# Averages over the channels from two float32r halves, and the next block's v product placed later: a retention and FFN layer on one Trainium2 core

## The chip, the cores and the metric

The kernel runs on one core of one Trainium2 chip (trn2). The metric is the device time of one execution in microseconds (us): the median of several runs, and beside it one execution taken with the hardware profiler. The engines are called as in the profile: PE is the matrix engine, PEld its weight load, DVE the vector engine, ACT the scalar engine, POOL GpSimd, and SP the engine whose queue issues nearly all DMAs.

## The reference, cut to what matters

The input has 4 sequences of 1024 tokens with 512 channels. All is float32; the FFN weights are first rounded to float8_e4m3fn.

```python
x = L0_attn_x
x = x + _layernorm(_L0_attn_ref(_layernorm(x), Wq, Wv, Wo, Wg, gamma, beta_ln, beta))
x = x + _layernorm(_L0_ffn_ref(_layernorm(x), gate_w, up_w, down_w, scales...))

# _L0_attn_ref(x)
q = (x @ Wq.T).reshape(Bsz, Ls, NHEAD, HEAD_DIM)
v = (x @ Wv.T).reshape(Bsz, Ls, NHEAD, HEAD_DIM)
ret = _retention_scan(v, lam)              # state = lam * state + v_t along the tokens
out = (q * ret).reshape(Bsz, Ls, D)
out = _layernorm(out, ln_gamma, ln_beta)   # mean and variance over the 512 channels
out = out * jax.nn.silu(x @ Wg.T)
return out @ Wo.T

# _L0_ffn_ref(x)
fuse = silu((x @ q8(gate_w)) * gate_scale) * ((x @ q8(up_w)) * up_scale)
return (fuse @ q8(down_w)) * down_scale
```

The change touches the mean and the variance of the inner `_layernorm(out, ...)`, and the order in which one v product is issued.

## The kernel before, in words

**Tiles.** The 4096 tokens are cut into 8 blocks of 512. For the attention half of a block (`class Retention`, line 316 and on) activations lie with channels on the 128 partitions: 512 channels are 4 chunks (`c`), and a tile of one chunk is 128x512. Each of q, v and g (`gate` of `Retention`, line 451) takes for each chunk four f32 products of 128x512 that add up in one PSUM tile (`project`, line 281). In the profile one f32 product is two rows. The scan along the tokens is one DVE instruction for each chunk (`scan`, line 393). `y_of` (line 412) multiplies q by the scanned v, and POOL adds the four chunks into `self.sum` (`ysum` in the profile).

**Mean and variance over the channels.** Channels lie on partitions and over four chunks. After POOL has summed the chunks, one f32 product with a 128x128 matrix of 1/512 (`mean_w`) sums over the partitions and gives each partition the mean (`mean`, line 425, PSUM tile `mu`). `center_y` (line 429) subtracts it from the four chunks on DVE, squares them on ACT, and POOL adds up the squares (`sqsum`). `var` (line 442) does the same product on these, and ACT takes the root; `rstd_y` (line 448) inverts it on DVE. `z` (line 465) then scales a chunk, shifts it and multiplies it by silu(g); `o` (line 477) is the output product.

**The FFN half** (`class Ffn`, line 533 and on) goes through 12 steps `i` of 128 inner channels. `gate` and `up` do eight float32r products each: the input was split into two float32r halves, an upper one made by an ACT cast and the rest by a DVE subtraction (`upper_of`, `rest_of`, lines 525 and 528), and each is multiplied by the rounded weights. `fuse` (line 557) multiplies gate and up on DVE and casts the upper half on ACT, `rest` subtracts the other half on DVE, and `down` does eight products two steps later.

**The order.** Every operation goes through `InOrder` (line 66), which keeps the program order on each engine; so every row of the profile names line 74, and rows are told apart by their tiles. The order is written out by hand in the loop of line 784: loop `t` runs the FFN of block t (`f`), and weaves into its 12 steps the rest of the FFN of block t−1 (`l`), the attention of block t+1 (`b`, there in loops 0 to 6) and the loading, normalizing and first products of block t+2 (`n`, there in loops 0 to 5). In steps 3 to 6 PE does `f.gate(i)`, then a group of g for `b`, then `f.up(i)`, then `f.down(i-2)`. In step 3 the mean of `b` stands ahead of that group, in step 4 the variance. In step 11 the first v chunk of `n` follows `f.gate(11)`.

```python
            if n and i == 11:
                n.v(0)
                n.scan(0)
            if n and i == 11:
                b.turn_x1n(3)
                b.upper_of(3)
            units()
            f.up(i)
            f.fuse(i)
```

The normalized input of `n` reaches this product through memory: DVE transposes 32x32 blocks (`send_x`, line 366), a DMA writes them (`mx`), and `fetch_x` (line 380, issued at the end of step 9, or 7 in loop 0) reads them back into `xnT`. The transposed FFN input of `b` goes a like way for three of four token groups (`move_x1n`); the fourth is turned on PE (`turn_x1n(3)`, tile `pt`). Loop 0 also rounds the FFN weights to float8 on DVE and ACT (`rounds`, line 221, and `units`, line 214; tiles `scr`). Loop 1 looks for weights out of range on ACT (`next(search)`; tile `seen`).

**Buffers.** PSUM: tag `pa` has two buffers, which v, q, g, mu, var, o and the transposes take in turn; `pf` has two for gate and up; `pd0` to `pd3` have one each for down. In SBUF, tag `ret` has two buffers (scanned v, squares, blocks to be transposed, search), tag `rstd` one (`ysum`, then `sqsum`, then the root), tag `sg` three (gates).

Of the kernel before, what the change touches and what calls it, by code (L numbers as in the profile page):

```python
# [10 lines left out]
F32 = mybir.dt.float32  # L11
I32 = mybir.dt.int32
F32R = mybir.dt.float32r
F8 = mybir.dt.float8e4
AF = mybir.ActivationFunctionType
ALU = mybir.AluOpType

P = 128
# [5 lines left out]
def retention_ffn_sandwich(  # L24
# [24 lines left out]
    TB = 512  # L49
# [5 lines left out]
    const = ctx.enter_context(tc.tile_pool(name="const", bufs=1))  # L55
# [3 lines left out]
    work = ctx.enter_context(tc.tile_pool(name="work", bufs=2))  # L59
# [6 lines left out]
    class InOrder:  # L66
# [9 lines left out]
    pe, dve, act, pool, sp = (  # L76
        InOrder(e) for e in (nc.tensor, nc.vector, nc.scalar, nc.gpsimd, nc.sync)
    )
# [49 lines left out]

    ident = const.tile([P, P], F32, tag="ident", name="ident")
    make_identity(nc, ident)  # L130
    mean_w = const.tile([P, P], F32, tag="mean_w", name="mean_w")
    dve.memset(mean_w, 1.0 / D)
    eps_sb = const.tile([P, 1], F32, tag="eps_sb", name="eps_sb")
    dve.memset(eps_sb, EPS)
# [79 lines left out]
    def units():  # L214

        while open_units:
            _, c = open_units.pop(0)
            act.activation(c, c, AF.Relu, bias=neg_low)
            act.activation(c, c, AF.Identity, scale=1.5 * 2.0**20, bias=low_unit)
# [41 lines left out]
    def rstd_in_place(var, n):  # L261
        pool.tensor_scalar(var, var, EPS, 1.0, ALU.add, ALU.mult)
        pool.tensor_tensor(var, var, nhalf[:, :n], ALU.pow)
# [30 lines left out]
    def ps_tile(name, home="pa"):  # L294
        return homes[home].tile([P, TB], F32, tag=home, name=name)
# [20 lines left out]
    class Retention:  # L316
# [24 lines left out]
        def shift(self):  # L341

            mean, rstd = self.mv[:, :, 0], self.mv[:, :, 1]
            pool.tensor_scalar(mean, mean, -1.0, 1.0, ALU.mult, ALU.mult)
            pool.tensor_tensor(mean, mean, rstd, ALU.mult)
# [76 lines left out]
                pool.tensor_tensor(self.sum, self.sum, y[:, c, :], ALU.add)  # L422


        def mean(self):
            self.mu = ps_tile(f"mu_{self.t}")
            pe.matmul(self.mu, mean_w, self.sum, start=True, stop=True)

        def center_y(self):

# [10 lines left out]

        def var(self):
            var = ps_tile(f"var_{self.t}")
            pe.matmul(var, mean_w, self.sum, start=True, stop=True)
            self.sum = work.tile([P, TB], F32, tag="rstd", name=f"rstd_{self.t}", bufs=1)
            act.activation(self.sum, var, AF.Sqrt, bias=eps_sb)

# [226 lines left out]
    b = Retention(1)  # L674
# [109 lines left out]
    for t in range(NB):  # L784
        f, n = Ffn(a), None
        for i in range(NI):
            if t > 0 and (t > 1 or i):
                (f if i else l).rest((i - 1) % NI)
            if t == 0 and i == 0:
                n = Retention(2)  # L790
# [44 lines left out]
            if l and b and i == 2:  # L835
                l.stats(0)
                l.stats(1)
            if b and i == 3:
                b.mean()
                b.center_y()  # L840
                if t == 0:
                    n.stats(3)
                    n.rstd()
                    n.shift()
                b.g_of(0)
            if b and i == 4:
                b.var()
                b.g_of(1)
                b.rstd_y()
            if b and i == 5:  # L850
                b.g_of(2)
                b.z(1)
# [14 lines left out]
                b.upper_of(i - 9)  # L867
            if b and 7 <= i <= 10:
                b.o_moments(i - 7)
            if n and i == 11:  # L870
                n.v(0)
                n.scan(0)
            if n and i == 11:
                b.turn_x1n(3)
                b.upper_of(3)
            units()
            f.up(i)
            f.fuse(i)
            if t == 0:
                if i < 8:  # L880
                    rounds(3, now=i == 3)
# [57 lines left out]
            if b and i == 4 and 0 < t < NB - 2:  # L939
                n = Retention(t + 2)  # L940
# [6 lines left out]
        l, a, b = f, b, n  # L947
# [70 lines left out]
```

## Time and profile before

| what | value |
|---|---|
| median of 3 runs | 1018.72 us (1018.16 to 1019.34) |
| the profiled execution, its own time | 1018.71 us |
| its span (first to last instruction) | 1016.9 us |
| TensorE clock granted, mean | 0.997 of full speed |
| DVE busy | 605.7 us in 931 instructions |
| ACT busy | 321.4 us in 475 instructions |
| POOL busy | 242.7 us in 290 instructions |
| g products (pg<-xnT,wg_sb), rows, busy | 256, 114.9 us |
| mu and var products, rows | 16 and 16 |

A row of the timeline has the start (from the span's start), the duration, the engine, the line, the operation with output and inputs, the shape and a count; the bracket at its end is idle time of the engine just before and what ended it. Rows of PE overlap, since products are pipelined: the cost of a group in a full stream is the distance from the end before to its own end. A row of waits gives the total, the number and the longest. The profiled execution is within the spread of the runs, and 1.8 us longer than its span.

### The profile page before, as it was taken

The page shows a single profiled execution, that of the slowest core. Times are in us where ns is not written, and L with a number is a line of the kernel's source. Part 1 is how long each engine was busy: PE and PEld are TensorE (multiplying, and loading weights), DVE is VectorE, ACT ScalarE, POOL GpSimd, SP SyncE. Part 2 cuts the span into 40 slices and gives each one's busy share as a digit, 9 for nine tenths or more (in the row PEclk, how much of TensorE's full clock was granted, in tenths as well). Part 3 has the DMA queues.
Part 4 walks back from the last instruction along what each step waited for, and adds up shares of the span by engine and source line. Part 5 has one row for each costly group of instructions (what it writes and reads, how often), then busy time and mean ns, then how long its engine had stood idle before and what let it go on. Part 6 is the DMA issues. An engine that isn't in the chain of part 4 may idle for free.

```text
span 1016.9 us, 9749 instructions
## 1 busy us (share of the span) xinstructions
PE 995.9 (98%) x3502; PEld 651.0 (64%) x3502; DVE 605.7 (60%) x931; ACT 321.4 (32%) x475; POOL 242.7 (24%) x290
## 2 busy tenths in 40 slices
PE   9999999999999999999999999999999999999997
PEld 6454766666665666666666566665666666666885
DVE  5996896435665465753657446573556735547444
ACT  3646574334754132111321113211141111412222
POOL 1405222214031140311413114130132302213021
PEclk9999999999999999999999999999999999999998
DMA  9212224301125022340204402052020510103021
GB/s 302 103 61 103 84 83 104 103 1 51 43 83 135 0 86 91 103 114 1 83 11 121 96 1 83 18 135 76 0 83 32 134 63 1 42 21 124 1 83 41
DMA packets 62608, 73.79 MB, mean 73 GB/s; under 512 B 5856, under 2 KB 36320, under 8 KB 62560
## 3 DMA queue, kind: packets, MB, share of 16 engines
q1 hardware_dynamic: 60976, 72.24, 23.2%
q10 hardware_dynamic: 1584, 0.94, 0.4%
q8 instruction: 27, 0.44, 0.2%
q14 instruction: 21, 0.17, 0.1%
HBM read 43.53 MB, written 29.62 MB: 72 GB/s over the span
## 4 chain that ended last, share of the span: by engine, by line
PE 87%; DMA 5%; DVE 4%; POOL 2%; ACT 1%; issue 1%; SPq 1%; POOLq 0%; DVEq 0%; ACTq 0%
PE pfu L74 16%; PE pfg L74 15%; PE pd L74 15%; PE pv L74 11%; PE pg L74 10%; PE pq L74 10%; PE po L74 8%; DMA xnT<-mx 3%; DVE xn L74 1%; DMA mx<-xn 1%; PE var L74 1%; PE mu L74 1%; SPq L74 1%; POOL x L74 1%; POOL sqsum L74 1%
## 5 line engine op out<-in xcount | busy, mean ns | idle before, releaser
L74 PE MATMUL pfu<-x1nT,up_sb 128*128 128x512 f32 x768 | 222.0, 431 | 0.0
L74 PE MATMUL pfg<-x1nT,gate_sb 128*128 128x512 f32 x768 | 190.4, 390 | 1.2 <-ACT x1nT L74 0.7
L74 PE MATMUL pd<-down_sb,fuse 128*128 128x512 f32 x720 | 188.3, 403 | 0.0
L74 PEld LDWEIGHTS pfu<-x1nT,up_sb 128*128 128x128 f32 x768 | 144.1, 188 | 61.1 <-issue 35.2
L74 PEld LDWEIGHTS pfg<-x1nT,gate_sb 128*128 128x128 f32 x768 | 143.9, 188 | 31.7 <-DVE x1nT L74 1.0
L74 PEld LDWEIGHTS pd<-down_sb,fuse 128*128 128x128 f32 x720 | 135.2, 188 | 38.0 <-issue 10.8
L74 ACT CAST fuse<-gate 128x512 fp32r<-128x512 f32 x90 | 55.9, 621 | 306.9 <-DVE gate L74 306.9
L74 DVE SCALAR_TENSOR_TENSOR gate<-pfu,us_sb,gate 128x512 f32<-128x512 f32 x96 | 71.7, 747 | 122.4 <-PE pfu L74 118.3
L74 ACT ACTIVATE gate<-pfg,gs_sb 128x512 f32<-128x512 f32 x96 | 65.9, 686 | 246.6 <-PE pfg L74 243.5
L74 PE MATMUL pv<-xnT,wv_sb 128*128 128x512 f32 (+1 forms) x280 | 115.2, 557 | 8.6 <-DMA xnT<-mx 7.0
L74 PE MATMUL pg<-xnT,wg_sb 128*128 128x512 f32 x256 | 114.9, 592 | 0.0
L74 PE MATMUL pq<-xnT,wq_sb 128*128 128x512 f32 x256 | 114.9, 592 | 0.0
L74 PE MATMUL po<-wo_sb,y 128*128 128x512 f32 x256 | 114.5, 592 | 0.0
L74 POOL TENSOR_SCALAR mv<-mv 128x1 f32<-128x1 f32 (+1 forms) x77 | 19.8, 257 | 331.2 <-DVE mv L74 330.5
L74 PEld LDWEIGHTS pv<-xnT,wv_sb 128*128 128x128 f32 x280 | 52.4, 189 | 57.2 <-issue 43.3
L74 PEld LDWEIGHTS pg<-xnT,wg_sb 128*128 128x128 f32 x256 | 48.5, 190 | 55.2 <-issue 53.4
L74 PEld LDWEIGHTS po<-wo_sb,y 128*128 128x128 f32 x256 | 48.4, 189 | 50.1 <-issue 47.7
L74 DVE TENSOR_TENSOR fuse<-gate,fuse 128x512 fp32r<-128x512 f32 x90 | 73.4, 815 | 11.7 <-ACT fuse L74 11.7
L74 PEld LDWEIGHTS pq<-xnT,wq_sb 128*128 128x128 f32 x256 | 48.3, 189 | 49.5 <-issue 47.4
L74 POOL TENSOR_TENSOR x<-x,x1n 128x512 f32<-128x512 f32 x32 | 49.1, 1534 | 45.9 <-DVE x1n L74 35.5
L74 DVE TENSOR_TENSOR_SCAN ret<-lam,pv 128x512 f32<-128x512 f32 x16 | 19.5, 1219 | 54.9 <-PE pv L74 52.4
L74 DVE BATCH_NORM_STATS2 st<-x 128x6 f32<-128x512 f32 x64 | 43.5, 680 | 13.8 <-POOL x L74 11.2
(104 smaller groups left out, 889.6 us busy)
## 6 DMA issues: line engine op xcount, KB each, us to landing
kept<-x SPq DMA_DIRECT2D x32, 256.0 KB, 2.1
x<-kept SPq DMA_DIRECT2D x32, 256.0 KB, 3.5
x<-in_x SPq DMA_DIRECT2D x28, 256.0 KB, 3.7
out<-d SPq DMA_DIRECT2D x27, 256.0 KB, 2.0
xnT<-mx SPq DMA_DIRECT2D x24, 256.0 KB, 4.7
mxs<-xs SPq DMA_DIRECT2D x84, 64.0 KB, 1.8
x1n<-mxs SPq DMA_DIRECT2D x21, 256.0 KB, 2.6
mx<-xn SPq DMA_DIRECT2D x20, 256.0 KB, 2.3
```

The source lines that it names most:

```text
L74: return lambda *args, **kwargs: tc.keep_in_program_order(op(*args, **kwargs))
```

## The change

The averages of blocks 1 to 7 are made from two float32r halves of the sum. ACT casts the sum (`hi`), DVE subtracts it from the sum (`lo`), and two float32r products with the same matrix of 1/512 add up in PSUM. Block 0 keeps the f32 product. The halves take the `ret` buffers. In steps 3 and 4 the group of g now stands ahead of the average on PE, and the halves are issued ahead of that group. `rstd_y` moves behind `f.up(4)` and `f.fuse(4)`. In step 11 the v product of `n`, its scan, the last transposes of `b` and their upper half move behind `f.up(11)` and `f.fuse(11)`.

```diff
-    mean_w = const.tile([P, P], F32, tag="mean_w", name="mean_w")
+    mean_r = const.tile([P, P], F32R, tag="mean_r", name="mean_r")
+    mean_w = mean_r.bitcast(F32)
     dve.memset(mean_w, 1.0 / D)
...
+        def halves(self):
+
+            self.hi, self.lo = (
+                work.tile([P, TB], F32R, tag="ret", name=f"half_{self.t}") for _ in range(2)
+            )
+            act.copy(self.hi, self.sum)
+            dve.tensor_tensor(self.lo, self.sum, self.hi, ALU.subtract)
+
+        def average(self, dst):
+            if self.t == 0:
+                pe.matmul(dst, mean_w, self.sum, start=True, stop=True)
+            else:
+                pe.matmul(dst, mean_r, self.hi, start=True, stop=False)
+                pe.matmul(dst, mean_r, self.lo, start=False, stop=True)
+
         def mean(self):
             self.mu = ps_tile(f"mu_{self.t}")
-            pe.matmul(self.mu, mean_w, self.sum, start=True, stop=True)
+            self.average(self.mu)
...
         def var(self):
             var = ps_tile(f"var_{self.t}")
-            pe.matmul(var, mean_w, self.sum, start=True, stop=True)
+            self.average(var)
...
             if b and i == 3:
+                b.halves()
+                b.g_of(0)
                 b.mean()
                 b.center_y()
                 if t == 0:
                     n.stats(3)
                     n.rstd()
                     n.shift()
-                b.g_of(0)
             if b and i == 4:
+                b.halves()
+                b.g_of(1)
                 b.var()
-                b.g_of(1)
-                b.rstd_y()
...
+            units()
+            f.up(i)
+            f.fuse(i)
+            if b and i == 4:
+                b.rstd_y()
             if n and i == 11:
                 n.v(0)
                 n.scan(0)
-            if n and i == 11:
                 b.turn_x1n(3)
                 b.upper_of(3)
-            units()
-            f.up(i)
-            f.fuse(i)
```

## The prediction, made before the changed kernel had run

> **What bounds the kernel now.** I read first the busy shares, then the waits of PE, then the timeline of the stretches that the edit touches.
>
> ```profile
> PE 995.9 (98%) x3502; PEld 651.0 (64%) x3502; DVE 605.7 (60%) x931; ACT 321.4 (32%) x475; POOL 242.7 (24%) x290
> ```
>
> PE's stream is the span: a microsecond taken out of it, or of its idle time, is a microsecond of the result, and no other engine matters unless PE comes to wait for it. The waits of PE (microseconds in total, times, longest) hold little:
>
> ```profile
> PE pv L74 <- DMA xnT<-mx: 7.0, 5, 1.5
> PE var L74 <- POOL sqsum L74: 0.9, 1, 0.9
> ```
>
> The 7.0 is block t+2's first v product in FFN step 11, in loops t=1 to 5 (1.48, 1.42, 1.32, 1.34, 1.48); loop 0 has no such wait. The 0.9 is block 0's variance at 50.5 us, before the loops, which the edit leaves alone. The timeline of step 11 in loop 5 (start, duration, engine, row):
>
> ```profile
> 809.00 1.97 PE L74 MATMUL pfg<-x1nT,gate_sb 128*128 128x512 f32 x8
> 812.45 3.67 PE L74 MATMUL pv<-xnT,wv_sb 128*128 128x512 f32 x8 [1.48 <-DMA xnT<-mx]
> 815.96 0.60 PE L74 MATMUL pt<-ident,x1n 128*128 128x128 f32 x4
> 816.16 1.28 DVE L74 TENSOR_TENSOR_SCAN ret<-lam,carry,pv 128x512 f32<-128x512 f32 x1 [2.58 <-DMA kept<-x]
> 816.32 2.11 PE L74 MATMUL pfu<-x1nT,up_sb 128*128 128x512 f32 x8
> 818.27 3.60 PE L74 MATMUL pq<-xnT,wq_sb 128*128 128x512 f32 x8
> ```
>
> To be seen: between v and q lie the transposes and the up products, and under them the scan, which reads v's PSUM buffer. Steps 3 and 4 of the same loop:
>
> ```profile
> 860.56 1.98 PE L74 MATMUL pfg<-x1nT,gate_sb 128*128 128x512 f32 x8
> 862.38 1.02 PE L74 MATMUL mu<-ysum,mean_w 128*128 128x512 f32 x2
> 863.24 3.60 PE L74 MATMUL pg<-xnT,wg_sb 128*128 128x512 f32 x8
> 863.44 2.48 DVE L74 TENSOR_TENSOR y<-y,mu 128x512 f32<-128x512 f32 x4 [1.04 <-PE mu L74]
> 865.46 4.01 POOL L74 TENSOR_TENSOR sqsum<-sqsum,sq 128x512 f32<-128x512 f32 x3 [0.71 <-ACT sq L74]
> 870.05 3.35 POOL L74 TENSOR_TENSOR d<-d,x 128x512 f32<-128x512 f32 x2 [0.57 <-DVE d L74]
> 870.31 1.98 PE L74 MATMUL pfg<-x1nT,gate_sb 128*128 128x512 f32 x8
> 872.13 1.02 PE L74 MATMUL var<-sqsum,mean_w 128*128 128x512 f32 x2
> 872.99 3.60 PE L74 MATMUL pg<-xnT,wg_sb 128*128 128x512 f32 x8
> ```
>
> Taking ends (start plus duration), PE goes 862.54, 863.40, 866.84: the mean costs 0.86, four f32 products of a group 3.44, eight float32r products 1.82 (0.2275 each). Loop 0 is different, since DVE also rounds weights there:
>
> ```profile
> 119.60 1.15 ACT L74 ACTIVATE scr<-scr,low_unit 128x1024 f32<-128x1024 f32 x1
> 120.79 2.45 DVE L74 TENSOR_TENSOR y<-y,mu 128x512 f32<-128x512 f32 x4
> 128.25 3.60 PE L74 MATMUL pg<-xnT,wg_sb 128*128 128x512 f32 x8
> 131.88 1.23 DVE L74 TENSOR_TENSOR up_sb<-scr 128x1024 fp32r<-128x1024 f32 x1
> 133.02 3.35 DVE L74 RECIPROCAL rstd<-rstd 128x512 f32<-128x512 f32 x1
> ```
>
> From 120.79 to 133.02 DVE runs without a gap: y, statistics, the step-3 gate product, then six rounding and rest operations.
>
> [...] 0.86 against 0.2275 is 3.8. [...] the fuse subtraction of 0.68 takes 1.78 at 809.50, ending 0.55 after POOL's addition of 809.07 to 810.73. [...]
>
> **The change, part by part.** The halves exist for blocks 1 to 7, so in loops 0 to 6: 14 averages.
>
> *Products.* One f32 product (0.86) becomes two float32r (0.455): −0.40 each if both halves are there in time. Each average adds an ACT cast (0.62, from fuse<-gate) and a DVE subtraction (0.68).
>
> *The mean, loops 1 to 6* (times of loop 5). The gate SiLU on ACT ends at 863.33, the high half 863.9; the low half waits at worst for POOL's d addition to end (864.75) and is there at 865.3. PE gets to it after the group, at 866. Nothing waits. Behind hi stand only the g SiLU and the squares. Centring starts at 866.5 instead of 863.44.
>
> *The variance, loops 1 to 6.* PE without waits: mean ends 866.44, up 868.26, down 870.08, gate 871.89, group 1 875.33; it needs the low half by 875.5. The chain: centring 866.5, first POOL sum 2.0 later at 868.5 as before. The norms and the rest subtraction now fall among the sums, which last took 4.01 alone; a blocked POOL addition ends 1.14 after release (871.03 to 872.17 in the d additions). I get ends 869.8, 871.6, 873.3. High half 874.0; [...] low half 875.25. Margin 0.25: no wait taken, bounds 0 and 1.3 (below). In loop 1 a search activation (1.56+0.19) puts hi at 874.8 and lo at 875.5: I take 0.2. Behind a waiting low half stand STT(4), the reciprocal and z; behind hi on ACT the g SiLU, root and cast.
> Loops 1 to 6: 12 × −0.40 + 0.2 = −4.6.
>
> *Loop 0.* In step 3 ACT finishes the rounding at 120.75, then hi 121.4, lo 122.1; PE, ready at 121.25, ends the mean near 122.5. Centring starts at 122.57 instead of 120.79, 1.78 late. The low half of the variance stands on DVE where the reciprocal stood, behind the same full queue: 133.02+1.78 = 134.8, done 135.4. PE wants it at about 131.6 and waits some 3.7. It ends the variance at 135.85, where before group 1 ended at 131.85: **+4.0**. Bounds: 2.3, if the rounding operations that POOL stretches (1.31 and 2.32 against 0.68 and 1.22) run free, and 4.8. Afterwards DVE's lateness against PE is only 0.8 more, and po of step 7 had 2.2 to spare (154.92 against z's 152.70).
>
> *rstd_y, g_of moved.* The reciprocal goes behind up's products, at 878.4 to 881.8; z(0), z(1) end by 885.4, before up(5) is done at 886.5. Cover: those 4.7 us; without it the 3.35 would fall on the gate product. The later d additions delay output and x loads on SP's queue by up to 2.5; the first statistics of that x come in step 5, 6 us after. Zero, bounds 0 and 0.5. PSUM: mean and group exchange buffers, each free long before.
>
> *v behind up.* Moved are four v products, scan and carry copy, four transposes and ACT's upper_of(3), past eight up products, the gate product and its cast. They issue no DMA, so SP's and POOL's queues stay. Gate ends 810.97, up 812.79; xnT was there by 812.45, so the 1.48 is covered, by 0.2 to 0.3. But what is late next is the scan: pq_0 takes pv_0's PSUM buffer (two buffers in turn, pv, pt, pq), and only the transposes are left to hide the scan. v ends 816.23, scan 816.27 to 817.55, q starts near 817.61 (0.06 after a DVE result, as pfg at 96.33) and ends, restarted, 3.67 later: 821.28 against 821.87. Gain 0.59; the same sum in loops 1 to 4 with scans of 1.28 or 1.22: 0.58, 0.53, 0.42, 0.49. Together −2.6. Loop 0 had no DMA wait: q ended 9.51 after gate, now 10.25: +0.7. Everything on PE queues behind this wait. The next gate needs rest_of(3), done near 819.1, at 823. Bounds of the whole move: −3.5 and +1.5.
>
> *Sum.* −4.6 + 4.0 − 2.6 + 0.7 = −2.5. The profiled execution took 1018.71 (span 1016.9, 1.8 around it), the median 1018.72: **1016.2**.
>
> **Rivals.** *Full gain*: 14 × 0.40 and all 7.0: 1018.7−12.6 = 1006.1. For it speaks the wait row; against it the PSUM turn and loop 0's queue. *Loop 0 waits less* (2.3): 1014.5. *The v move gives nothing*, xnT landing 0.4 late or q restarting slowly: 1018.7−4.6+4.0 = 1018.1 to 1018.8. *Low halves partly late*, 0.3 to 0.65 in six loops: 1018.0 to 1020.1; for it speaks the 0.25 margin. *Slower*: [...] lo 876.6, PE ends the variance at 877.05 instead of 875.79: 1.26 × 6 = 7.6, 1023.8. It decides from 0.76 a loop (4.6/6). Against it: DVE at 809.50 got in at the end of one POOL operation. *The change doesn't do what it says*: float32r averages at f32 pace, 1.26 more for each of 12: 1031; against it speaks pfu's 0.2275.
>
> **Numbers.** About 0.2% (2.0 us) is what a measurement can tell from no change. Forecast 0.50 (own range 1015.2 to 1017.2; 0.38 of it below 1016.7), less waiting in loop 0 0.12, full gain 0.03, low halves partly late 0.20, v move nothing 0.05, slower 0.08, pace 0.02. Faster 0.38+0.12+0.03 = 0.53, same 0.12+0.25 = 0.37, slower 0.10. Range 1014.0 to 1020.0, which leaves out full gain, the two slower cases and edges.
>
> **What would show it.** PE pv's DMA wait gone; in its place q waiting for the scan (ret or carry), six times about 1.0; one PE wait for a half in loop 0 near 3.7; mu and var rows from the halves, 14 each, at the float32r duration (0.39); POOL's sqsum sums longer than 4.01. It is wrong if var waits appear in loops 2 to 6, if q does not wait, or if loop 0 shows no wait.

## The result and the profile after

| | before | changed |
|---|---|---|
| median | 1019.15 us (1018.16 to 1021.35, 14 runs) | 1019.17 us (1018.18 to 1021.44, 14 runs) |
| ratio, with its 95% interval | | 1.0001 (0.9993 to 1.0009) |
| profiled execution, span | 1018.71, 1016.9 | 1021.44, 1019.7 |

No difference can be measured. The changed kernel's profiled execution is the slowest of its runs, so the medians are compared for the time, and the profile is used for where it goes. The first line of the page, then the waits of PE:

```profile
PE 995.2 (98%) x3502; PEld 654.1 (64%) x3502; DVE 635.3 (62%) x945; ACT 328.3 (32%) x489; POOL 242.6 (24%) x290
```

```profile
PE pq L74 <- DVE ret L74: 5.5, 6, 1.0
PE var L74 <- DVE half L74: 4.4, 2, 3.7
...
PE mu L74 <- DVE half L74: 0.2, 1, 0.2
```

The wait for xnT (7.0) is gone. Two others stand in its place: q for the scan in the six loops 0 to 5, and the variance for its low half, once for 3.7 us (loop 0) and once for 0.7 (loop 1).

To see where the time went I took the end of each of the 96 gate groups in both timelines and subtracted. The difference moves at few places (us; minus is time gained):

| place | profile after minus before | predicted |
|---|---|---|
| ahead of loop 0 | +1.38 | 0 |
| loop 0, mean | +0.47 | } 4.0 |
| loop 0, variance | +6.65 | } |
| loop 1, mean, variance | −0.41, +0.59 | −0.40, −0.2 |
| loops 2 to 6, each average | −0.41 (ten times) | −0.40 |
| v move, loop 0 | +0.72 | +0.7 |
| v move, loops 1 to 5 | −0.52, −0.52, −0.40, −0.52, −0.59 | −0.58, −0.53, −0.42, −0.49, −0.59 |

The 1.38 lies ahead of anything that the edit moves. The experiments below have the same start and show −0.45 to +0.67 there, so it is a matter of the single execution and is left out. From loop 0 on the profile shows +1.35. Step 11 in loop 5 of the changed kernel, the stretch shown of before:

```profile
813.13 1.98 PE L74 MATMUL pfg<-x1nT,gate_sb 128*128 128x512 f32 x8
814.95 1.98 PE L74 MATMUL pfu<-x1nT,up_sb 128*128 128x512 f32 x8
...
816.76 3.59 PE L74 MATMUL pv<-xnT,wv_sb 128*128 128x512 f32 x8
...
820.19 0.60 PE L74 MATMUL pt<-ident,x1n 128*128 128x128 f32 x4
...
820.40 1.28 DVE L74 TENSOR_TENSOR_SCAN ret<-lam,carry,pv 128x512 f32<-128x512 f32 x1 [2.02 <-PE pv L74]
...
821.73 3.70 PE L74 MATMUL pq<-xnT,wq_sb 128*128 128x512 f32 x8 [0.94 <-DVE ret L74]
```

v starts with no idle time in its bracket. The scan ends at 821.68, and q starts 0.05 later, after 0.94 of idle time: the scan has then read v, and q can take v's PSUM buffer. Steps 3 and 4 of the same loop:

```profile
865.62 2.67 POOL L74 TENSOR_TENSOR d<-d,x 128x512 f32<-128x512 f32 x2 [0.42 <-issue]
...
865.92 3.59 PE L74 MATMUL pg<-xnT,wg_sb 128*128 128x512 f32 x8
...
867.41 1.44 DVE L74 TENSOR_TENSOR half<-ysum,half 128x512 fp32r<-128x512 f32 x1 [1.46 <-ACT half L74]
868.95 1.03 PE L74 MATMUL mu<-half,mean_r 128*128 128x512 f32 x2
...
872.11 4.14 POOL L74 TENSOR_TENSOR sqsum<-sqsum,sq 128x512 f32<-128x512 f32 x3 [3.81 <-ACT sq L74]
...
876.21 3.40 POOL L74 TENSOR_TENSOR d<-d,x 128x512 f32<-128x512 f32 x2
876.28 0.62 ACT L74 CAST half<-sqsum 128x512 fp32r<-128x512 f32 x1
876.93 1.54 DVE L74 TENSOR_TENSOR half<-sqsum,half 128x512 fp32r<-128x512 f32 x1
878.29 1.03 PE L74 MATMUL var<-half,mean_r 128*128 128x512 f32 x2
```

Both subtractions (`half<-ysum,half` and `half<-sqsum,half`) take about 1.5 us in place of 0.68, and both overlap POOL's d additions; the first ends at 868.85, 0.56 after POOL's row of 865.62. The second ends at 878.47, when PE is in the first of its two products: no idle time shows, but next to nothing is to spare. Loop 0, where PE waits longest:

```profile
132.74 0.50 PE L74 MATMUL var<-half,mean_r 128*128 128x512 f32 x1
...
135.09 1.23 DVE L74 TENSOR_TENSOR up_sb<-scr 128x1024 fp32r<-128x1024 f32 x1
...
136.23 0.68 DVE L74 TENSOR_TENSOR half<-sqsum,half 128x512 fp32r<-128x512 f32 x1
136.97 0.80 PE L74 MATMUL var<-half,mean_r 128*128 128x512 f32 x1 [3.73 <-DVE half L74]
137.56 3.62 PE L74 MATMUL pfu<-x1nT,up_sb 128*128 128x512 f32 x8
...
140.98 3.00 PE L74 MATMUL pd<-down_sb,fuse 128*128 128x512 f32 x8
```

The low half comes right behind the rounding, and the wait is 3.73. But look at the rows after it: eight up products take 3.62 and not 1.98, with nothing in a bracket. The reason is in the granted clock (the column after POOL's) of the stretches around:

```profile
core 0: us, PE busy (x) PEld busy (x) DVE busy (x) ACT busy (x) POOL busy (x), PEclk, DMA share, GB/s
122.00:132.70 10.70, 10.40 (x36) 6.31 (x34) 9.61 (x14) 7.61 (x12) 6.34 (x5) 1.00 0.13 48
132.70:137.00 4.30, 0.57 (x3) 0.22 (x2) 4.18 (x6) 1.88 (x2) 3.52 (x3) 0.92 0.37 122
137.00:139.50 2.50, 2.50 (x6) 2.02 (x7) 0.00 (x0) 1.70 (x2) 0.00 (x0) 0.50 0.61 210
139.50:142.00 2.50, 2.50 (x7) 1.92 (x7) 0.78 (x2) 1.17 (x2) 0.00 (x0) 0.50 0.00 0
142.00:144.00 2.00, 2.00 (x8) 1.58 (x7) 2.00 (x1) 0.62 (x1) 0.00 (x0) 0.72 0.00 0
```

PE runs at half its clock. The 0.92 and the 0.72 of the stretches at the edges place the half clock from about 136.3 to 143.1: 6.8 us, of which PE has products for the last 6.1. In the kernel before the clock is 1.00 in the same step.

### The profile page after: what moved, and what is told of

The parts are those of the page before. It is cut to its first block, busy times and chain, and to the rows that moved or that the text cites. A ratio compares the mean times of both kernels' runs of the same rounds, so it can differ in the third digit from the quotient of the medians.

```text
span 1019.7 us, 9800 instructions
## 1 busy us (share of the span) xinstructions
PE 995.2 (98%) x3502; PEld 654.1 (64%) x3502; DVE 635.3 (62%) x945; ACT 328.3 (32%) x489; POOL 242.6 (24%) x290
## 4 chain that ended last, share of the span: by engine, by line
PE 91%; DVE 4%; POOL 2%; ACT 1%; issue 1%; DMA 1%; ACTq 0%; POOLq 0%; DVEq 0%
PE pfu L74 17%; PE pfg L74 17%; PE pd L74 17%; PE pv L74 11%; PE pq L74 10%; PE po L74 10%; PE pg L74 9%; DVE ret L74 1%; DVE scr L74 1%; DMA x<-in_x 1%; POOL sqsum L74 1%; POOL x L74 0%; PE var L74 0%; POOL mv L74 0%; PE mu L74 0%
## 5 line engine op out<-in xcount | busy, mean ns | idle before, releaser
L74 PE MATMUL pfu<-x1nT,up_sb 128*128 128x512 f32 x768 | 217.2, 425 | 0.0
L74 DVE TENSOR_TENSOR fuse<-gate,fuse 128x512 fp32r<-128x512 f32 x90 | 79.4, 883 | 6.9 <-ACT fuse L74 6.9
```

What stands on the lines that cost most here:

```text
L74: return lambda *args, **kwargs: tc.keep_in_program_order(op(*args, **kwargs))
```

## The experiments

**Theory.** The small gains are there (averages −0.41, v move −1.8), and loop 0 takes them back: through DVE's queue ahead of the low half, and through the clock, which falls to 0.50 by the idle time of 3.73 us. **Rivals:** the slow products come from loop 0's other work and not from the idle time; one of the two parts gains and the other loses; the v move was held by something other than the scan. Each kernel was timed against the kernel before on the same chip.

### Filling the idle time: e1_filled

```diff
                 pe.matmul(dst, mean_r, self.hi, start=True, stop=False)
+                if self.t == 1 and fill:
+                    busy = ps_tile("busy", "pf")
+                    for _ in range(fill):
+                        pe.matmul(busy[:, :P], mean_w, mean_w, start=True, stop=True)
                 pe.matmul(dst, mean_r, self.lo, start=False, stop=True)
...
-            self.average(var)
+            self.average(var, 15)
```

> 15 idle products of 128x128 (their result is never read) stand on PE between the two halves of block 1's variance, where PE waits 3.7 us in the changed kernel. Theory (the idle time lets PE's clock fall, which costs 2.6 us on top of the wait): step 4 of loop 0 costs 4.0 us over the kernel before in place of 6.65, the clock stays at 1.00 there, the up products of step 4 take 1.8 us and not 3.6. Rival (the slow products come from the load of loop 0, memory transfers or the rounding, not from the idle time): step 4 stays at 6.6 us and the clock falls to 0.5 again. In time: theory about 1.2 us under the kernel before if the clock falls in every execution of the changed kernel; rival no difference from it.

Measured: 1017.34 us (1016.82 to 1018.41, 13 runs) against 1018.70; ratio 0.9989 (0.9980 to 0.9997). The timeline of the place:

```profile
131.71 0.50 PE L74 MATMUL var<-half,mean_r 128*128 128x512 f32 x1
132.06 3.51 PE L74 MATMUL busy<-mean_r 128*128 128x128 f32 x30
135.94 0.50 PE L74 MATMUL var<-half,mean_r 128*128 128x512 f32 x1 [0.38 <-DVE half L74]
136.28 2.00 PE L74 MATMUL pfu<-x1nT,up_sb 128*128 128x512 f32 x8
138.12 1.98 PE L74 MATMUL pd<-down_sb,fuse 128*128 128x512 f32 x8
```

```profile
132.00:136.00 4.00, 3.62 (x32) 3.39 (x31) 3.85 (x5) 1.88 (x2) 3.19 (x3) 1.00 0.42 131
136.00:140.00 4.00, 4.00 (x18) 3.31 (x19) 1.68 (x2) 3.39 (x4) 0.00 (x0) 1.00 0.45 135
```

The low half comes as late as before, the clock stays at 1.00, up takes 2.00, and step 4 costs 3.79 in place of 6.65. The memory traffic and the rounding are still there, so here the idle time is what costs the clock (0.50 with it, 1.00 with the gap filled), and 6.65−3.79 = 2.86 us is its price in that profile. In the medians the difference is half of that (1.36 us under the kernel before against none), so the fall costs less in most executions.

The granted clock tells how much less. The next experiment, e2, has the same wait of 3.73 us, and its profile shows the half clock for one stretch of 3.41 us only:

```profile
135.31:136.26 0.95, 0.95 (x4) 0.82 (x5) 0.00 (x0) 0.41 (x1) 0.00 (x0) 1.00 0.23 70
136.26:139.67 3.41, 3.41 (x10) 2.64 (x9) 0.89 (x2) 2.57 (x4) 0.00 (x0) 0.50 0.38 134
139.67:142.00 2.33, 2.33 (x11) 1.92 (x11) 2.33 (x1) 0.51 (x1) 0.00 (x0) 1.00 0.00 0
```

Half of 3.41 is 1.7; e2's step 4 costs 5.40−3.79 = 1.6 more than with the gap filled. The mean clock of every execution is on record as well. It is 0.997 to 0.999 in all 13 runs of e1 and in 43 of the 45 of the kernel before timed with it, and 0.994 to 0.997 in the 14 of the changed kernel: 0.994 or 0.995 in its three slowest (1020.45 to 1021.44 us), 0.996 or 0.997 in the others. By estimate one stretch of 3.41 us at half clock takes 0.0017 off the mean, and two take 0.0033. By that estimate the clock falls in most or all executions of the changed kernel, for one stretch in the eleven and for two in the three, of which the profiled one is the slowest.

### Each part alone: e2_averages_only and e3_v_only

In e2 the step-11 lines stand as before, ahead of `f.up(i)`; in e3 the averages are those of before:

```diff
 # e2_averages_only
+            if n and i == 11:
+                n.v(0)
+                n.scan(0)
+                b.turn_x1n(3)
+                b.upper_of(3)
             units()
             f.up(i)
             f.fuse(i)
             if b and i == 4:
                 b.rstd_y()
-            if n and i == 11:
-                n.v(0)
-                n.scan(0)
-                b.turn_x1n(3)
-                b.upper_of(3)
```

> The averages from halves alone; v stays ahead of up in step 11. Theory: eleven averages gain 0.41 each, loop 1's variance loses 0.6, loop 0 loses 4.5 without a fall of the clock and 7.1 with it: 0.6 to 3.2 us over the kernel before. The five waits for xnT come back, 7.0 us, and q waits for no scan. Rival (the averages gain and the v move loses): 2 us or more under the kernel before.

Measured: 1020.79 us (1019.60 to 1024.42, 19 runs) against 1018.70; ratio 1.0019 (1.0013 to 1.0026). Step 4 of loop 0 costs 5.40, the averages of loops 2 to 6 give −0.41 each, loop 1's variance +0.57. PE's first two waits:

```profile
PE pv L74 <- DMA xnT<-mx: 5.7, 4, 1.5
PE var L74 <- DVE half L74: 4.4, 2, 3.7
```

The old wait for xnT is back (the fifth time, 1.2 us, is put down to another releaser), and the averages alone lose 2.1 us.

> The v move alone, averages in f32 as before. Theory: five loops gain 0.52, 0.52, 0.40, 0.52 and 0.59 us, loop 0 loses 0.72, since q waits for the scan some 0.9 us in each of six: 1.8 us under the kernel before. Rival (the v move covers the whole wait, and something of the averages takes it back): 6 to 7 us under. Rival (the v move loses): over the kernel before.

Measured: 1016.95 us (1016.43 to 1017.72, 19 runs) against 1018.70; ratio 0.9983 (0.9977 to 0.9990). Its steps: +0.72, −0.51, −0.51, −0.43, −0.48, −0.59, together −1.8, and all else from loop 0 on within 0.03. Its longest wait is the scan's:

```profile
PE pq L74 <- DVE ret L74: 5.5, 6, 1.0
```

So the v move gains 1.8 alone. It neither covers the whole wait of 7.0 nor loses.

### Block 1 without halves: e4_block1_f32

```diff
-            if self.t == 0:
+            if self.t < 2:
                 pe.matmul(dst, mean_w, self.sum, start=True, stop=True)
...
             if b and i == 3:
-                b.halves()
-                b.g_of(0)
+                if t > 0:
+                    b.halves()
+                    b.g_of(0)
                 b.mean()
                 b.center_y()
                 if t == 0:
                     n.stats(3)
                     n.rstd()
                     n.shift()
+                    b.g_of(0)
             if b and i == 4:
-                b.halves()
-                b.g_of(1)
+                if t > 0:
+                    b.halves()
+                    b.g_of(1)
                 b.var()
+                if t == 0:
+                    b.g_of(1)
+                    b.rstd_y()
...
-            if b and i == 4:
+            if b and i == 4 and t > 0:
                 b.rstd_y()
```

> As the changed kernel, but block 1 (loop 0) keeps the f32 average and its place ahead of the group of g. Theory: loop 0's loss of 4.5 to 7.1 us goes and nothing else changes: eleven averages at 0.41, loop 1's variance +0.6, the v move -1.8: 5.7 us under the kernel before. Rival (DVE's queue in loop 0 is delayed by something else of the change, or the clock falls there anyway): a loss in steps 3 to 5 of loop 0 stays.

Measured: 1012.79 us (1012.50 to 1013.36, 5 runs) against 1018.70; ratio 0.9943 (0.9929 to 0.9957). Loop 0 shows +0.02 in all apart from the v move; the other places are those of the changed kernel. The halves of loop 0, with the order that goes with them (g ahead of the average, `rstd_y` behind up), are the whole loss of 7.1.

### Why the low half is late in loop 0: e7_low_half_early

On the changed kernel:

```diff
-            if t == 0 and i == 4:
-                rounds(3, now=False)
...
             if b and i == 4:
                 b.halves()
+                if t == 0:
+                    rounds(3, now=False)
                 b.g_of(1)
```

> The changed kernel with one edit: in step 4 of loop 0 the three rounding operations that stood ahead of the low half on DVE stand behind it. Theory (the low half is late through its place in DVE's queue): it is there some 3.0 us earlier, PE waits about 0.7 in place of 3.7, the clock does not fall, step 4 costs about 1.0 in place of 6.65: 4 to 4.5 us under the kernel before. Rival (the chain through ACT and POOL is as late as the queue): the wait stays over 2 us.

Measured: 1013.85 us (1013.38 to 1014.33, 5 runs) against 1018.72; ratio 0.9953 (0.9940 to 0.9965). Step 4 costs 0.84, the mean still 0.44.

```profile
131.04 0.49 PE L74 MATMUL var<-half,mean_r 128*128 128x512 f32 x1
131.53 0.68 DVE L74 TENSOR_TENSOR half<-sqsum,half 128x512 fp32r<-128x512 f32 x1
...
132.27 0.50 PE L74 MATMUL var<-half,mean_r 128*128 128x512 f32 x1 [0.74 <-DVE half L74]
132.60 2.00 PE L74 MATMUL pfu<-x1nT,up_sb 128*128 128x512 f32 x8
```

The same work, in another order on DVE, gives back 5.8 us of step 4: the queue was the cause. The time is 4.9 us under the kernel before, a little more than the 4 to 4.5 expected. The wait of 0.74 is not followed by slow products: up takes 2.00.

### The scan's wait: e5_down_first

On e4_block1_f32:

```diff
-            if n and i == 11:
-                n.q(0)
-                n.y_of(0)
-
             if i == f.lag:
                 f.sums()
             if f.lag <= i < (NI if b else NI - 1):
                 f.down(i - f.lag)
             elif l and i < 2:
                 l.down(NI - 2 + i)
+            if n and i == 11:
+                n.q(0)
+                n.y_of(0)
```

> As e4_block1_f32, but in step 11 the down products of the step stand ahead of q. Theory (q waits for the scan only because nothing but four transposes stands between v and q): the eight down products (1.8 us) cover the 0.9 us wait in each of six loops, the wait for ret goes, 5.5 us under e4, that is 11.4 us under the kernel before. Rival (q's PSUM buffer is free later than the scan's end, or something else comes late next, such as y_of(0) or the next gate's input): part of the wait stays or comes up at pfg or pq of the next step.

Measured: 1005.63 us (1005.53 to 1005.78, 4 runs) against 1018.72; ratio 0.9872 (0.9858 to 0.9885). Each against the kernel before on its chip, that is 7.2 under e4 and not 5.5; between the two profiles step 11 makes 7.0.

```profile
805.57 0.60 PE L74 MATMUL pt<-ident,x1n 128*128 128x128 f32 x4
805.77 1.28 DVE L74 TENSOR_TENSOR_SCAN ret<-lam,carry,pv 128x512 f32<-128x512 f32 x1 [2.01 <-PE pv L74]
805.92 2.09 PE L74 MATMUL pd<-down_sb,fuse 128*128 128x512 f32 x8
...
807.86 3.59 PE L74 MATMUL pq<-xnT,wq_sb 128*128 128x512 f32 x8
```

The scan lies under the down products, and no wait for ret is left: the v move had been held by the scan alone. Step 11 gains 1.1 to 1.3 a loop where the waits were 0.92 on average. The rows of PE show where the rest lies. In the stream q starts 0.15 before the row ahead of it has ended (807.86 against 805.92+2.09 = 808.01) and takes 3.59; behind the wait, in the changed kernel, it starts after the 0.94 and takes 3.70. So that wait cost 0.94+0.15+0.11 = 1.20, and the row of waits counts only the 0.94.

### Loop 1: e6_search_later

On e5_down_first:

```diff
-            for _ in range(look[i] // 2 if t == 1 else 0):
+            for _ in range(look[i] // 2 if t == 1 and i != 4 else 0):
                 next(search)
...
                 b.var()
+                if t == 1:
+                    next(search)
```

> As e5_down_first, but in step 4 of loop 1 the search activation stands behind the root on ACT and not ahead of the high half. Theory (that activation makes the halves of block 2's variance late by 0.7 us): step 4 of loop 1 goes from +0.6 to -0.4 against the kernel before, 1.0 us under e5. Rival ([...] 1.46 us for 0.68): less than half of it goes.

Measured: 1005.03 us (1004.65 to 1005.64, 4 runs) against 1018.72; ratio 0.9864 (0.9849 to 0.9879). That is 0.6 under e5 where 1.0 was expected. The interval overlaps e5's, and only the profile separates the two: step 4 of loop 1 goes from +0.59 to −0.41. Loop 1 in the changed kernel, then here:

```profile
259.98 1.56 ACT L74 ACTIVATE seen<-gate_sb,neg_max 128x1536 fp8e4<-128x1536 f32 x1
260.14 2.94 POOL L74 TENSOR_TENSOR d<-d,x 128x512 f32<-128x512 f32 x2
...
262.17 1.46 DVE L74 TENSOR_TENSOR half<-sqsum,half 128x512 fp32r<-128x512 f32 x1 [1.45 <-ACT half L74]
...
263.69 0.50 PE L74 MATMUL var<-half,mean_r 128*128 128x512 f32 x1 [0.68 <-DVE half L74]
```

```profile
251.21 3.40 POOL L74 TENSOR_TENSOR d<-d,x 128x512 f32<-128x512 f32 x2
251.28 0.62 ACT L74 CAST half<-sqsum 128x512 fp32r<-128x512 f32 x1
251.93 1.54 DVE L74 TENSOR_TENSOR half<-sqsum,half 128x512 fp32r<-128x512 f32 x1
253.30 1.03 PE L74 MATMUL var<-half,mean_r 128*128 128x512 f32 x2
```

The subtraction is as slow as before (1.54 here, 1.46 in the changed kernel), but starts in time. The rival, that its slowness alone is the cause, falls. This version has the lowest median here, 13.7 us under the kernel before.

## Why the prediction was right or wrong, step by step

The time is 3.0 us above the forecast and within its range. Against the kernel before timed with it, nothing is there of the 2.5 us that were to be gained, though a gain had been given the larger chance. That the time still lies in the range is in part luck: the upper part of the range stood for low halves that come late in six loops and for a v move that gives nothing. Neither happened (a low half came late in one of the six loops only), and the cost that did come, a fall of the clock, has no term in the prediction.

- *Products* and *the mean, loops 1 to 6*: right. −0.41 where −0.40 stood.
- *v behind up*: right in mechanism and size. DMA wait gone, q waiting for the scan in its place, −1.83 where −1.9 stood; e3 shows it alone, e5 shows that the scan was what held q. Had the row of waits been taken for the gain, −7 would have stood here.
- *Loop 0*: this term was mis-sized, 4.0 where 7.1 was measured. The mechanism, DVE's queue ahead of the low half, and the wait (3.7 foretold, 3.73 found) were right, as e7 and e4 show. What failed was taking a wait to cost only its own length: with 3.73 us of idle time PE's clock fell to 0.50, and the following products took 2.86 longer in that profile. With the gap filled (e1) loop 0 costs 0.46+3.79 = 4.25, close to the 4.0 of the sum. The granted clock was 0.50 with the wait of 3.73 (changed kernel, e2) and 1.00 with the gap filled (e1); after the wait of 0.74 (e7) up took 2.00. The half clock lasted 6.83 us in the changed kernel's profile and 3.41 in e2's, so the same wait of 3.73 cost 2.86 on top of its length in the one and 1.6 in the other. In the changed kernel's profile the clock fell 0.69 ahead of the wait's end, in e2's 0.95 behind it, when PE was at work again. What sets the moment of the fall and its length was not shown.
- *The variance, loop 1*: mis-sized, −0.2 where +0.59 was measured. The mechanism, the search activation ahead of the high half, was right (e6). I had POOL's sums stretched to about 4.8, and the low half between two d additions. The sums took 4.14, so POOL was already in the second d addition when the low half came.
- *The variance, loops 2 to 6*: no wait, as said. The slow subtraction beside POOL's d additions that was foreseen is there (1.54 where it took 0.68 in loop 0), and the margin, 0.25 in the prediction, was about zero. That the low half would be held up by a d addition was the author's estimate, from the one subtraction of 1.78 in the kernel before.
- *The sum*: −2.5, with +3.1 for loop 0 and +0.8 for loop 1 instead, makes +1.4. The profile shows +1.35 from loop 0 on, and the median none. The distance between them is the length of the half clock: with the 1.6 of one stretch of 3.41 in place of the 2.86 of two, +1.35 becomes +0.1 by estimate, and one stretch is what the clocks of eleven of the 14 executions fit.

## What to carry to other kernels

Before a product is moved behind another to hide its wait, look at who must read its buffer before the next product can start: here the scan had stood under the very products that were moved away, and one more exchange (down ahead of q) was worth more than the move itself (7.2 us against 1.8). An edit that is right in the steady loops can lose all of it in the one loop whose queues are full, so each loop that differs wants its own sum. Here a wait cost more than its length: the one of 3.73 us, with which PE's clock fell to 0.50, cost 2.86 us more in one profile and 1.6 in another.

## What the runs showed of the hardware that was not expected

- With a wait of 3.73 us PE's granted clock was 0.50 for 6.83 us in one profile (changed kernel) and for 3.41 in another (e2); at half clock eight float32r products took 3.62 where they took 2.00 in the same step of e1 and e7. After the gap of 0.74 (e7) they took 2.00, and in loops 1 to 5 of the changed kernel, with gaps of up to 1.0 ahead of q, the clock was 1.00.
- The clock fell 0.69 us ahead of the end of that wait in the changed kernel and 0.95 behind it in e2, when PE had products again.
- Removing six waits of 0.92 (5.5 in all) gained 7.2 us in the medians and 7.0 in the profiles.
- The DVE subtraction that makes a low half took 1.39 to 1.54 in loops 1 to 6, where POOL was adding d at the time, and 0.68 to 0.69 in loop 0, where it was not.
